# A recurrent scan on one core: one tanh per stream's step, 64-column state products, and a fixed order on PE

## The chip, the cores and the metric

The kernel runs on 1 core of a Trainium2 chip. The metric is device time in microseconds (us) of one execution. All arithmetic is fp32. In the trace every fp32 matrix product appears as two LDWEIGHTS and two MATMUL instructions, called its two passes here.

## The reference

The whole program is four layers of attention-like mixing and mixture-of-experts on 8 sequences of 256 tokens with 128 features. The change lies in the first layer's mixing alone, a nonlinear recurrence with 16 heads of 64 states and 8 features:

```
def _L0_attn_ref(tokens, norm_w, a, b, c, skip, w_out, b_out):
    ...
    x = tokens * jax.lax.rsqrt(ms + EPS) * norm_w
    x = x.reshape(B, T, H, D)            # 8, 256, 16, 8
    a_t = jnp.tanh(a)                    # 16 heads, 64 x 64
    state0 = jnp.zeros((B, H, S), dtype=tokens.dtype)

    def step(state, x_t):
        state = jnp.tanh(jnp.einsum('bhs,hst->bht', state, a_t) + jnp.einsum('bhd,hds->bhs', x_t, b))
        mixed = jnp.einsum('bhs,hsd->bhd', state, c) + skip[None] * x_t
        return (state, mixed)
    ...
    _, outs = jax.lax.scan(step, state0, xs)
    ...
    return tokens + outs @ w_out.T + b_out
```

The 256 steps are strictly one after another: each needs the tanh of the one before. The state of a step is 8 x 16 x 64 numbers. All later layers work on the normalised sum that this layer gives, so none of them can start before the scan's results are there.

## The kernel before, in words

The tokens are held in four groups of 512 (`g` of `NG`). `l0_attn` loads its weights, takes the tanh of `a`, clears the state tiles (L188), scales and transposes the tokens (L190 to L209) into `xd` (the input of the products, spread over head pairs) and `xnT` (for the skip term), and then runs the scan.

The 16 heads are arranged as 8 stacks of two heads. A stack's two heads share the 128 partitions: 64 states of one, 64 of the other. Stacks 0 to 3 are stream `h` = 0, stacks 4 to 7 stream `h` = 1; the two streams are independent, so that one can be on PE while the other is on ACT. Even and odd steps (`u`) pair the heads in two different ways, so that what leaves the products of one step has the arrangement that the next one needs.

A block is 16 steps (`TB`). For each block and stream a PSUM bank (`us`, pool `ps_s`, four banks) holds the sums of 16 steps.

- Input products (L224): for a block, 32 products with 32 output columns (a quarter of the array, `cols`) and 128 moving columns write b times x for all 16 steps at once.
- State products (L239): in each step and stream, eight products of 128 x 32 weights (half a head's features of one stack each) with 16 moving columns, added to the same bank. Four of them stand side by side on the four column quarters of PE's array.
- Tanh (L248): two ACTIVATEs of 64 partitions x 32 elements per step and stream. Each writes only the half of the partitions and the half of the state tile that its head owns; the other halves stay zero from the memset, which makes the state block-diagonal and keeps a stack's two heads apart in a 128-row product.
- Output products (L259): after a block, 16 products with 32 output columns and 128 moving columns give c times the state for the block, into `pm` in a bank of a lane's pool `ps`.
- DVE adds the skip term (L269, L270), and after the scan L280 multiplies `outsT` with the output weights.

What order the instructions take on an engine is decided by a scheduler, which works with its own estimate of each instruction's duration; the program's text only gives the dependencies. So before the change the input and output products stand between the state products wherever the scheduler saw room, often 20 and more in a row. `tc.add_manual_dep`, wrapped by `behind`, adds an order by hand; before the change it is used for some DMAs alone. Behind the scan come the router and the experts of the first layer (L301 and L306 are their products, L308 their gate), further attention layers, and the routed experts (L565 and L575 their products, L569 their gate).

Of the kernel before, what the change touches and what calls it, by code (L numbers as in the profile page):

```python
# [42 lines left out]
def tile_post_ln_blocks(ctx: ExitStack, tc: tile.TileContext, I, out: bass.AP):  # L43
# [10 lines left out]
    def bank(pool):  # L54
        return pool.tile([P, 512], F32, tag=pool.name, name=pool.name)
# [103 lines left out]
    def l0_attn(x):  # L159

        TB = 16
        cols = [slice(32 * c, 32 * c + 32) for c in range(4)]
        low, high = slice(0, 64), slice(64, 128)
        with ExitStack() as es:
            wp = es.enter_context(tc.tile_pool(name="l0w", bufs=1))
            wk = es.enter_context(tc.tile_pool(name="l0k", bufs=2))
            a_sb = load(wp, "L0_a")  # L170
            b_sb = load(wp, "L0_b")
            c_sb = load(wp, "L0_c")
            normw = load(wp, "L0_norm_w")
            normd = load(wp, "L0_norm_d")
            skip = load(wp, "L0_skip")
            woT = load(wp, "L0_w_outT")
            bout = load_row(wp, "L0_b_out")
            S.activation(a_sb, a_sb, AF.Tanh)

            xnT = wp.tile([P, T // 2, 2, B], F32, tag="xnT", name="xnT")  # L180
            xd = wp.tile([P, T // 2, 2, 2, B], F32, tag="xd", name="xd")
            outsT = wp.tile([P, B, T], F32, tag="outsT", name="outsT")
            states = []
            for h in range(2):
                states.append([])
# [24 lines left out]

            ps_m = es.enter_context(tc.tile_pool(name="ps_s", bufs=4, space=bass.MemoryType.PSUM))
            prev = [None, None]
            for blk in range(T // TB):
                ts = slice(blk * TB // 2, (blk + 1) * TB // 2)
                st = [states[h][blk % 2] for h in range(2)]
# [4 lines left out]
                for u in range(2):  # L220
                    for h in range(2):
                        for s in range(2):
                            for c in range(4):
                                PE.matmul(  # L224
                                    us[h][cols[c], s, u].rearrange("p t e b -> p t (e b)"),
                                    lhsT=b_sb[:, u, 4 * h + 2 * s + c // 2, 32 * (c % 2) : 32 * (c % 2) + 32],
                                    rhs=xd[:, ts, u, :, :].rearrange("p t e b -> p t (e b)"),
                                    start=(u == 0 and s == 0),
                                    stop=False,
                                    skip_group_check=True,  # L230
                                )
                for t in range(TB):
                    v, u = t // 2, t % 2
                    for h in range(2):
                        if prev[h] is not None:
                            for s in range(2):
                                for c in range(4):
                                    k = 2 * s + c // 2
                                    PE.matmul(  # L239
                                        us[h][cols[c], s, u, v].rearrange("p e b -> p (e b)"),  # L240
                                        lhsT=a_sb[:, u, 4 * h + k, 32 * (c % 2) : 32 * (c % 2) + 32],
                                        rhs=prev[h][:, k].rearrange("p e b -> p (e b)"),
                                        start=False,
                                        stop=(t == TB - 1),
                                        skip_group_check=True,
                                    )
                        for e, half in enumerate((low, high)):
                            S.activation(  # L248
                                st[h][half, v, u, :, e, :].rearrange("p (s k) b -> p s k b", s=2),
                                us[h][half, :, u, v, :, :],  # L250
                                AF.Tanh,
                            )
                        prev[h] = st[h][:, v, u]

                pm = bank(lanes[blk % 2].ps)[:, : TB * 2 * B].rearrange("p (u t e b) -> p u t e b", u=2, t=TB // 2, e=2)
                for u in range(2):
                    for k in range(2):
                        for q, c in enumerate(cols):
                            PE.matmul(  # L259
                                pm[c, u].rearrange("p t e b -> p t (e b)"),  # L260
                                lhsT=c_sb[:, u, 2 * q + k, :],
                                rhs=st[q // 2][:, :, u, 2 * (q % 2) + k].rearrange("p t e b -> p t (e b)"),
                                start=(u == 0 and k == 0),
                                stop=(u == 1 and k == 1),
                                skip_group_check=True,
                            )
                for u in range(2):
                    o = outsT[:, :, blk * TB : (blk + 1) * TB].rearrange("p b (t u) -> p t u b", u=2)[:, :, u]
                    V.scalar_tensor_tensor(o, xnT[:, ts, u], skip, pm[:, u, :, 0], ALU.mult, ALU.add)  # L269
                    V.tensor_tensor(o, pm[:, u, :, 1], o, ALU.add)  # L270

            for g in range(NG):
                xb = wk.tile([P, 4, D], F32, tag="sq", name="xb")
                V.scalar_tensor_tensor(
                    xb, x[g], 2.0, bout.unsqueeze(1).to_broadcast([P, 4, D]), ALU.mult, ALU.add
                )
                ps = quarters(bank(lanes[g % 2].ps))
                for j in range(4):
                    i = 4 * g + j
                    PE.matmul(  # L280
                        ps[:, j, :],
                        lhsT=outsT[:, i // 2, (i % 2) * P : (i % 2) * P + P],
                        rhs=woT,
                        start=True,
                        stop=True,
                    )
                V.tensor_tensor(xb, ps, xb, ALU.add)
                mixed(lanes[g % 2], g, xb)
# [1097 lines left out]
```

## Time and profile before

| what | us |
|---|---|
| median of 3 runs | 2330.99 |
| lowest and highest of them | 2328.26, 2331.98 |
| the profiled execution's own time | 2149.32 |
| its span, first to last instruction | 2147.6 |
| PE busy in the span | 1785.1 (83%) |
| ACT busy in the span | 950.8 (44%) |
| DVE busy in the span | 1267.9 (59%) |
| mean granted TensorE clock in the span | 0.872 |

The profile is one execution; its own time is some 182 us below the three runs. Busy shares are averages over stages with different limits. In a line for a group of instructions stand the source line, the engine, the operation, what it writes and reads with partitions x elements, the count, then busy us and mean ns of one, then the idle time of the engine just before them and what ended most of it. PEld is PE's weight load, listed by itself. The ends of matmuls are modelled, since they run in a pipeline.

### The profile page before, as it was taken

To read this page: it belongs to the slowest core of one execution; us is meant where nothing else is said; L and a number is where in the kernel's file an instruction comes from. 1 tells how busy PE (TensorE), PEld (TensorE's weight loads), DVE (VectorE), ACT (ScalarE), POOL (GpSimd) and SP (SyncE) were. 2 spreads that over 40 slices of the span, in tenths; PEclk is the share of its full clock that TensorE was granted. 3 is DMA by queue.
4 is the path that set the end of the run, shared out by engine and by line. 5 is a ranking of instruction groups with operands and counts; after the bars stand their busy time and mean duration, and the time that the engine had idled before them with its cause. 6 is when DMAs were issued, how large, how long until landed. Compare 5 with 4: busy or idle time off the path is not lost.

```text
span 2147.6 us, 46517 instructions
## 1 busy us (share of the span) xinstructions
PE 1785.1 (83%) x18200; PEld 1188.6 (55%) x18200; DVE 1267.9 (59%) x4476; ACT 950.8 (44%) x2385; POOL 290.4 (14%) x307
## 2 busy tenths in 40 slices
PE   5888878997899999999879762676975989998787
PEld 4666654455555544654458541554753766665564
DVE  3000016586786765689636851565667988477754
ACT  5666664372464435652333310243432554444424
POOL 1000000000000000003731067721047000000000
PEclk8666668997899999999879975798996999999958
DMA  3000006950233352235479795787731000000000
GB/s 94 5 5 5 5 4 192 270 165 0 62 96 81 87 149 75 63 82 160 119 248 315 232 274 180 237 283 226 209 91 51 1 1 1 1 6 6 1 1 11
DMA packets 186523, 219.66 MB, mean 102 GB/s; under 512 B 52896, under 2 KB 132256, under 8 KB 186304
## 3 DMA queue, kind: packets, MB, share of 16 engines
q1 hardware_dynamic: 163136, 164.24, 26.4%
q0 software_dynamic: 12800, 33.57, 5.1%
q10 hardware_dynamic: 10368, 18.88, 2.3%
q8 instruction: 143, 2.34, 0.5%
q14 instruction: 76, 0.62, 0.1%
HBM read 152.07 MB, written 64.55 MB: 101 GB/s over the span
## 4 chain that ended last, share of the span: by engine, by line
PE 60%; DVE 11%; ACT 9%; DMA 8%; POOL 6%; issue 5%; SPq 0%; ACTq 0%; POOLq 0%; DVEq 0%
PE ps_o L301 8%; PE ps_m L306 7%; PE ps_m L311 5%; ACT st L248 5%; PE ps_s L239 4%; PE ps L128 4%; PE ps L1002 3%; POOL got L586 3%; POOL placed L484 3%; PE ps L996 3%; PE ps_o L575 2%; DMA got<-in_F_w_dram,ei 2%; DMA got<-made,pl 2%; PE ps_s L224 2%; PE ps L1122 2%
## 5 line engine op out<-in xcount | busy, mean ns | idle before, releaser
L239 PE MATMUL ps_s<-st,L_a 128*32 128x16 f32 x8160 | 200.9, 206 | 45.1 <-ACT st L248 22.4
L248 ACT ACTIVATE st<-ps_s 64x32 f32<-64x32 f32 x1024 | 196.5, 192 | 92.8 <-PE ps_s L239 59.2
L308 ACT ACTIVATE h<-ps_m 128x512 f32<-128x512 f32 x196 | 116.1, 597 | 241.8 <-PE ps_m L306 222.3
L239 PEld LDWEIGHTS ps_s<-st,L_a 128*32 128x32 f32 x8160 | 159.2, 134 | 89.7 <-ACT st L248 72.3
L306 PE MATMUL ps_m<-xT,wg 128*128 128x512 f32 x384 | 197.8, 598 | 7.5 <-ACT h L308 7.5
L301 PE MATMUL ps_o<-h,wd 128*128 128x512 f32 x384 | 197.6, 599 | 7.0 <-DVE h L314 7.0
L455 POOL DMA_INDIRECT got<-in_F_w_dram,ei x32 | 30.7, 959 | 1121.4 <-DVE ei L442 971.4
L269 DVE SCALAR_TENSOR_TENSOR outsT<-xnT,L_skip,ps 128x64 f32<-128x64 f32 x32 | 10.3, 323 | 272.1 <-PE ps L259 255.5
L314 DVE TENSOR_TENSOR h<-h,bc 128x512 f32<-128x512 f32 x192 | 131.3, 686 | 45.9 <-ACT h L308 39.1
L484 POOL DMA_INDIRECT placed<-x,pl x128 | 126.3, 986 | 121.6 <-DVE pl L480 83.2
L586 POOL DMA_INDIRECT got<-made,pl x128 | 122.7, 959 | 126.3 <-DMA made<-ob 87.6
L311 PE MATMUL ps_m<-xT,wu 128*128 128x512 f32 x256 | 135.0, 609 | 4.1 <-ACT h L308 3.7
L575 PE MATMUL ps_o<-w,h 64*64 64x128 f32 x1152 | 94.0, 310 | 42.1 <-DVE h L570 29.2
L301 PEld LDWEIGHTS ps_o<-h,wd 128*128 128x128 f32 x384 | 72.1, 192 | 92.7 <-issue 62.5
L306 PEld LDWEIGHTS ps_m<-xT,wg 128*128 128x128 f32 x384 | 71.0, 191 | 91.7 <-issue 65.0
L312 DVE TENSOR_TENSOR h<-h,ps_m 128x512 f32<-128x512 f32 x132 | 90.0, 682 | 48.7 <-PE ps_m L311 43.7
L575 PEld LDWEIGHTS ps_o<-w,h 64*64 64x64 f32 x1152 | 73.7, 153 | 60.1 <-DVE h L570 41.6
L996 PE MATMUL ps<-nT,A_w 128*128 128x512 f32 x192 | 97.9, 623 | 10.1 <-DVE hT L998 7.3
L1002 PE MATMUL ps<-A_w,hT 128*128 128x128 f32 x768 | 101.1, 287 | 4.0 <-DVE hT L998 4.0
L1002 PEld LDWEIGHTS ps<-A_w,hT 128*128 128x128 f32 x768 | 95.2, 200 | 15.5 <-DVE hT L998 7.9
L565 PE MATMUL ps_m<-xg,w 128*64 128x64 f32 x1152 | 57.9, 252 | 50.2 <-DMA w<-further 22.7
L577 ACT COPY ob<-ps_o 128x512 f32<-128x512 f32 x72 | 42.2, 586 | 127.2 <-PE ps_o L575 124.9
(356 smaller groups left out, 3617.4 us busy)
## 6 DMA issues: line engine op xcount, KB each, us to landing
bc<-comb SPq DMA_DIRECT2D x128, 256.0 KB
placed<-zero SPq DMA_DIRECT2D x72, 256.0 KB
xb<-placed SPq DMA_DIRECT2D x72, 256.0 KB
made<-ob ACTq DMA_DIRECT2D x72, 256.0 KB
further<-got SPq DMA_DIRECT2D x32, 512.0 KB
w<-in_F_wg_dram SPq DMA_DIRECT2D x40, 256.0 KB
w<-in_F_wd_dram SPq DMA_DIRECT2D x40, 256.0 KB
bc<-comb SPq DMA_DIRECT2D x16, 512.0 KB
```

What stands on the lines that cost most here:

```text
L239: PE.matmul(us[h][cols[c], s, u, v].rearrange("p e b -> p (e b)"), lhsT=a_sb[:, u, 4 * h + k, 32 * (c % 2) : 32 * (c % 2) + 32], rhs=prev[ ...
L248: S.activation(st[h][half, v, u, :, e, :].rearrange("p (s k) b -> p s k b", s=2), us[h][half, :, u, v, :, :], AF.Tanh,)
L301: PE.matmul(acc[g], lhsT=w, rhs=h, start=begin, stop=end, skip_group_check=True)
L306: PE.matmul(pg, lhsT=wg, rhs=xT[g], start=True, stop=True)
L308: gate = S.activation(h, pg, func).ins
L311: PE.matmul(pu, lhsT=wu, rhs=xT[g], start=True, stop=True)
L314: V.tensor_tensor(h, h, bc[:, i * GT : (i + 1) * GT], ALU.mult)
L484: i = G.indirect_dma_start(placed[h][:, :], bass.IndirectOffsetOnAxis(rw[:, j, c : c + 1], 0), x[g][:, j, :], None).ins
L575: PE.matmul(po[k, i // 2, :], lhsT=h[k, i // 2, :], rhs=wd[k, i // 2, :], start=True, stop=True)
L586: G.indirect_dma_start(got[:, c, :], None, made[g // 2][:, :], bass.IndirectOffsetOnAxis(row[g][:, j, c : c + 1], 0))
L996: PE.matmul(ph, lhsT=w1[:, f * P : (f + 1) * P], rhs=nT, start=True, stop=True)
L1002: PE.matmul(po[:, j, :], lhsT=hT[:, f, j * P : (j + 1) * P], rhs=w2[:, f, :], start=(f == 0), stop=(f == 3),)
```

## The change

- The state tile of a stream and block has 2056 columns instead of 1024: each group of 8 columns that a head owns (`z` = 1) now has 8 columns of zeros ahead of it (`z` = 0), and 8 zeros close the tile.
- A stack's state product takes all 64 features of a head in one: 128 x 64 weights and 32 moving columns, on one of two halves of PE's array (`sides`). The moving columns are a window on the state tile that starts 8 columns later for one half than for the other, so that each half's own head meets numbers and the other meets zeros. There are four such products per step and stream.
- Since the sums of the foreign head are zero, one tanh of 128 partitions x 64 elements serves a stream's step.
- A bank now holds 8 steps (`HB`), and its 16 input products have 64 output columns and 64 moving columns.
- The first step too runs its state products, on a zero state.
- PE's order in the scan is written out: `in_turn` puts every state, input and output product behind the one before. In each step come stream 0's four products, two input products for the next half block, stream 1's four products, and after every fourth step four output products of the block before. The last block's outputs follow after the scan.

```diff
         TB = 16
         cols = [slice(32 * c, 32 * c + 32) for c in range(4)]
-        low, high = slice(0, 64), slice(64, 128)
+        sides = [slice(0, 64), slice(64, 128)]
...
-                    t = wp.tile([P, TB // 2, 2, 4, 2, B], F32, tag=f"st{h}{k}", name=f"st{h}{k}")
+                    t = wp.tile([P, TB * 4 * 32 + 8], F32, tag=f"st{h}{k}", name=f"st{h}{k}")
                     (V if h else G).memset(t, 0.0)
...
+            HB = TB // 2
+            def inputs(n):
                 us = [
-                    bank(ps_m).rearrange("p (s u t e b) -> p s u t e b", s=2, u=2, t=TB // 2, e=2)
+                    bank(ps_m).rearrange("p (t u s e f b) -> p t u s e f b", t=HB // 2, u=2, s=2, e=2, f=2)
                     for h in range(2)
                 ]
...
+                def product(u, h, s, c):
+                    return PE.matmul(
+                        us[h][sides[c], :, u, s, :, c, :],
+                        lhsT=b_sb[:, u, 4 * h + 2 * s + c, :],
+                        rhs=xd[:, n // 2 : (n + HB) // 2, u, :, :],
+                        start=(u == 0 and s == 0),
+                        stop=False,
+                        skip_group_check=True,
+                    )
...
+            def outputs(blk):
...
+                def product(u, k, q):
+                    return PE.matmul(
+                        pm[cols[q], u],
+                        lhsT=c_sb[:, u, 2 * q + k, :],
+                        rhs=st[q // 2][:, :, u, 2 * (q % 2) + k, :, 1, :],
...
+                def finish():
...
+            us, todo = inputs(0)
+            for f in todo:
+                f()
+            last = None
+            def in_turn(m):
+                nonlocal last
+                if last is not None:
+                    behind(m.ins, last, "steps in turn")
+                last = m.ins
+            outs, finish = [], None
+            prev = [states[h][1][:, (TB - 1) * 128 :] for h in range(2)]
+            for n in range(T):
+                t, blk = n % TB, n // TB
+                if t == 0 and blk:
+                    outs, finish = outputs(blk - 1)
+                if n % HB == 0:
+                    now, ins = us, []
+                    if n + HB < T:
+                        us, ins = inputs(n + HB)
+                for h in range(2):
+                    for s in range(2):
+                        for c in range(2):
+                            k = 2 * s + c
+                            in_turn(PE.matmul(
+                                now[h][sides[c], n % HB // 2, n % 2, s].rearrange("p e f b -> p (e f b)"),
+                                lhsT=a_sb[:, n % 2, 4 * h + k, :],
+                                rhs=prev[h][:, 32 * k + 8 * (1 - c) : 32 * k + 8 * (1 - c) + 32],
+                                start=False,
+                                stop=(n % HB == HB - 1),
+                                skip_group_check=True,
+                            ))
+                    st = states[h][blk % 2]
+                    S.activation(
+                        st[:, t * 128 : t * 128 + 128].rearrange("p (k e z b) -> p k e z b", k=4, e=2, z=2)[:, :, :, 1],
+                        now[h][:, n % HB // 2, n % 2].rearrange("p s e f b -> p (s e) f b"),
+                        AF.Tanh,
+                    )
+                    prev[h] = st[:, t * 128 : t * 128 + 136]
+                    if h == 0:
+                        more, ins = ins[:2], ins[2:]
+                    else:
+                        more, outs = (outs[:4], outs[4:]) if n % 4 == 3 else ([], outs)
+                    for f in more:
+                        in_turn(f())
+                    if finish and not outs:
+                        finish()
+                        finish = None
+            outs, finish = outputs(T // TB - 1)
+            for f in outs:
+                f()
+            finish()
...
```

In the changed file the state products are line 297, the tanh line 306, the input products line 224 still, the output products line 250, and DVE's two operations for them lines 262 and 263; everything behind the scan lies 54 lines further down.

More of the change, by code (lines that the diff above doesn't have):

```diff
@@ L211, in l0_attn @@
             ps_m = es.enter_context(tc.tile_pool(name="ps_s", bufs=4, space=bass.MemoryType.PSUM))
[L212 to L215, printed above, removed]
+            HB = TB // 2
+            def inputs(n):
                 us = [
-                    bank(ps_m).rearrange("p (s u t e b) -> p s u t e b", s=2, u=2, t=TB // 2, e=2)
+                    bank(ps_m).rearrange("p (t u s e f b) -> p t u s e f b", t=HB // 2, u=2, s=2, e=2, f=2)
@@ L218, in l0_attn @@
                     for h in range(2)
                 ]
[L220 to L264, printed above, removed]
-                                skip_group_check=True,
-                            )
@@ L267, in l0_attn @@
[L267 to L270, printed above, removed]
+                def product(u, h, s, c):
[7 more added lines that the diff above has]
+                    )
@@ new lines, in inputs @@
+                todo = [
+                    (lambda a=(u, h, s, c): product(*a))
+                    for u in range(2) for h in range(2) for s in range(2) for c in range(2)
+                ]
+                return us, todo
+            def outputs(blk):
+                st = [states[h][blk % 2][:, : TB * 4 * 32] for h in range(2)]
+                st = [t.rearrange("p (t u k e z b) -> p t u k e z b", t=TB // 2, u=2, k=4, e=2, z=2) for t in st]
+                pm = bank(lanes[blk % 2].ps)[:, : TB * 2 * B].rearrange(
+                    "p (u t e b) -> p u t e b", u=2, t=TB // 2, e=2
+                )
+                ts = slice(blk * TB // 2, (blk + 1) * TB // 2)
+                def product(u, k, q):
[3 more added lines that the diff above has]
+                        rhs=st[q // 2][:, :, u, 2 * (q % 2) + k, :, 1, :],
+                        start=(u == 0 and k == 0),
+                        stop=(u == 1 and k == 1),
+                        skip_group_check=True,
+                    )
+                def finish():
+                    for u in range(2):
+                        o = outsT[:, :, blk * TB : (blk + 1) * TB].rearrange("p b (t u) -> p t u b", u=2)[:, :, u]
+                        V.scalar_tensor_tensor(o, xnT[:, ts, u], skip, pm[:, u, :, 0], ALU.mult, ALU.add)
+                        V.tensor_tensor(o, pm[:, u, :, 1], o, ALU.add)
+                return [
+                    (lambda a=(u, k, q): product(*a)) for u in range(2) for k in range(2) for q in range(4)
+                ], finish
@@ new lines, in l0_attn @@
+            us, todo = inputs(0)
[27 more added lines that the diff above has]
+                                stop=(n % HB == HB - 1),
+                                skip_group_check=True,
+                            ))
[4 more added lines that the diff above has]
+                        AF.Tanh,
+                    )
+                    prev[h] = st[:, t * 128 : t * 128 + 136]
[8 more added lines that the diff above has]
+                        finish = None
```

## The prediction

> **What bounds the kernel now.** I read the page's table of slices first, then busy time by stretch, then the chain of waits inside the scan, last the groups of instructions that resemble the new ones.
>
> ```profile
> PE   5888878997899999999879762676975989998787
> PEclk8666668997899999999879975798996999999958
> ...
> L239 PE MATMUL ps_s<-st,L_a 128*32 128x16 f32 x8160 | 200.9, 206 | 45.1 <-ACT st L248 22.4
> L248 ACT ACTIVATE st<-ps_s 64x32 f32<-64x32 f32 x1024 | 196.5, 192 | 92.8 <-PE ps_s L239 59.2
> ```
>
> A slice is 53.7 us, so slices 2 to 6 are the scan: PE looks busy, but its rows count latency, ACT is busy for 0.6 of them by the same table, and the granted clock is 0.6. By the timeline its first tanh starts at 28.91 and its last ends at 315.38: 286.5 us, or 1.119 us for each of 256 steps. Nothing else of weight runs there, and every later stage needs its result, so a microsecond taken from the scan is one taken from the span. Two pieces of the chain show what a plain step is made of, at full and at half clock (start, length, what; us):
>
> ```profile
> 103.66 0.20 ACT st L248
> 103.86 0.02 issue
> 103.88 0.20 ACT st L248
> 104.08 0.02 issue
> ```
>
> ```profile
> 73.24 0.46 PE ps_s L239 x16
> 73.70 0.02 issue
> 73.72 0.02 ACTq L248
> 73.74 0.04 issue
> 73.79 0.20 ACT st L248
> 73.98 0.02 issue
> 74.00 0.20 ACT st L248
> 74.20 0.04 issue
> ```
>
> At full clock the tanh follow each other with no PE between (the next at 104.10 and 104.31, the next step's first at 104.57): ACT is the bound, 0.91 us a step. At half clock it is one stream's own loop: 0.46 (PE's 16 passes, two for each of 8 products) + 0.09 (issue, and a separate wait for ACT's own semaphore) + 0.42 (two tanh) + 0.04 = 1.01. The other 0.15 us of the mean step comes from the input and output products, which stand in clumps. So the clock matters. Each stretch below is about one step of the granted clock (stretch, length, PE busy (x), PEld busy (x), DVE, ACT, POOL, PEclk, DMA):
>
> ```profile
> 32.61:36.02 3.41, 2.54 (x128) 1.75 (x128) 0.00 (x0) 2.84 (x16) 0.00 (x0) 1.00 0.02 5
> 131.59:135.00 3.41, 3.08 (x118) 2.72 (x114) 0.00 (x0) 2.14 (x12) 0.00 (x0) 0.50 0.02 5
> 138.42:141.83 3.41, 2.66 (x133) 2.00 (x126) 0.00 (x0) 2.56 (x14) 0.00 (x0) 1.00 0.03 7
> 312.50:315.91 3.41, 3.28 (x78) 2.34 (x80) 0.00 (x0) 1.49 (x8) 0.00 (x0) 0.50 0.02 5
> ```
>
> The first was followed by half clock, the third by full; the second stayed at half, the fourth rose. Busy time doesn't sort them; the share in which moving columns stream does. A pass of 512 columns takes 0.43 us at full clock (L306: two passes in 0.86 in the chain), so 0.84 ns a column, 1.68 at half; four column tiles share the array. First: 128 x 16/4 x 0.84 = 0.43 of 3.41, 0.13. Third (100 passes of L239, 33 of L224 with 128 columns): 0.36. Second (92 of L239, 25 of L259): 0.57 at half. Fourth (48 of L239, 28 of L259, 2 of L280): 0.66. So the clock falls somewhere between shares 0.13 and 0.36 and rises between 0.57 and 0.66.
>
> **The change part by part.** Sums are against the profiled execution: 2149.32 us, span 2147.6. The median of the runs shown is 2330.99, 8.5% more; no view shows where those 182 us lie. The gain in them lies between the plain difference and one stretched by 1.085.
>
> *Tanh.* Two of 64x32 become one of 128x64. L248 takes 192 ns for 32 elements, and
>
> ```profile
> L569 ACT ACTIVATE h<-ps_m 128x256 f32<-128x256 f32 x72 | 27.7, 384 | 111.5 <-PE ps_m L565 91.0 <-DMA A_w<-in_A_w_dram 4.6 <-DMA made<-ob 4.1
> ```
>
> 384 for 256, so 64 take about 0.22 us: 0.20 less in each stream's loop, and ACT needs 0.5 us a step with its waits, no longer a bound. The separate wait stays (448 of 512 tanh wait on PE and on ACT; before, 450 of 1024).
>
> *State products.* Eight products of 32 columns with 16 moving become four of 64 with 32, so 8 passes in four pairs. The twin is L565, 128x64 weights with 64 moving, at full clock:
>
> ```profile
> 1107.59 0.68 PE L565 MATMUL ps_m<-xg,w 128*64 128x64 f32 x14
> ```
>
> ```profile
> 1107.16 0.25 PEld L575 LDWEIGHTS ps_o<-w,h 64*64 64x64 f32 x4
> 1107.59 0.54 PEld L565 LDWEIGHTS ps_m<-xg,w 128*64 128x64 f32 x14 [0.17 <-issue]
> ```
>
> 0.68 less the last pass's 0.22 is 0.46 for eight pairs: 0.058 a pair, set by the weights. Four pairs with the first load put the last start near 0.20; with a pass's 0.20 and the 0.04 that PE's piece in the chain ends after it, 0.44 against 0.46 before at half clock. The loop becomes 0.44 + 0.09 + 0.22 + 0.04 = 0.79 us. Bounds for the burst, 0.37 (no pacing) and 0.50 (every pair at twice): 18 us of scan down, 15 up.
>
> *Fixed order.* Each step now issues: stream 0's burst, two input products, stream 1's burst, and after every fourth step four output products. Bursts hold PE 0.20 each, the inputs 0.12 (two pairs at 0.058): 0.52 of 0.79, which fits. Each burst's first load waits for its own tanh; behind a waiting stream 1 stands stream 0's next burst, which isn't due before 0.79, so that costs nothing. Outputs do: they use 32-column tiles between bursts of 64. The weight loader idles 0.17 with no releaser as L575 (64x64) gives way to L565 (128x64) above; some 0.09 of it is after L575's columns have streamed. [...] From stream 1's last start (0.33 + 0.20): 0.03 streaming + 0.09 + 0.25 (a load, two passes of 128 columns) + 0.09 puts the next burst at 0.99 instead of 0.79: 0.05 us a step. [...] In the scan's tail a switch to 128x128 at half clock idles the loader 0.38, which would give 0.10. I take 0.05: 0.84 us a step, 215 us for 256.
>
> *Start and end.* The four memsets double (DVE 0.91 to 1.8 each, POOL 0.94 to 1.9), and DVE takes two xb operations (1.3 for both) earlier. Most hides behind the load of norm_d, which ends at 16.28, and the scaled copies of ACT; the last copies wait 0.97 for DVE already, so I add 1.5 (0 to 3). Of the input products only 16 stand ahead of the first burst, 32 passes or 1.7 us at half clock from 25.57: the first burst is at 28.8. Until the clock rises, 1.5 more. The end is 28.8 + 1.5 + 215 = 245 against 315.4: 70 us saved. The last block's outputs and DVE's four operations follow as before; the other blocks' DVE work hides in the scan, and if it didn't, a block's 1.2 us would show. No DMA, SP or POOL queue of the scan is moved.
>
> *Behind the scan.* The scheduler issues the same work; PE's order is unchanged up to about half of its later instructions (routed experts of the second half), then some shift by up to 61 places; SP swaps a few loads for later layers with the zeroing of placed. I count 0, with 15 us either way.
>
> Profiled execution: 2149 - 70 = 2079. Median: 2331 - 70 to 2331 - 76; I say 2258.
>
> **The rivals.**
>
> *The clock stays at half (slower).* Then pairs are 0.116 apart: burst 0.69 to its end, loop 1.04, but PE itself needs 0.42 + 0.23 + 0.42 = 1.07 a step, and outputs with two drains 0.86 in four: 1.29 a step, 330 us, so 44 more than now: about 2376. Streaming per step is 8 x 32 state + 128 input + 64 output columns = 448, 0.75 us at half clock: a share of 0.58, just where the trace shows neither sure rise nor stay. At full clock it is 0.377/0.84 = 0.45, above the 0.36 that stayed. So it is bistable, and the first burst decides: with 1.7 us of inputs in a 3.41 us window the share is about 0.75 if all lie in one, below 0.6 if split. The decisive point is a step of 1.12, some 60% of the scan at half. For a rise: any window that catches more inputs and outputs than average passes 0.62, and one rise is enough. [...]
>
> *Half in part.* Falls in some blocks, as now: a mean step near 1.0, 256 us, 30 saved less the start: 2303.
>
> *PE's order saves nothing, later stages lose.* If the new loop were 0.79 but every burst waited for the inputs ahead of it (0.12 twice) and the reordered tail lost 15: 1.08 a step, 10 saved, 15 lost, 2336. The 0.52 of 0.79 speaks against it.
>
> **How the numbers follow.** Full clock 0.75: 2258, own range 2220 to 2300 (18 burst, 13 drains, 15 tail, partly added). Half in part 0.12: 2303. Half throughout 0.09: 2376. Nothing gained 0.04: 2336. Range 2215 to 2325: it leaves out the half-clock case, the last one and the ends of the first. Faster by over 0.2%, about what a measurement of this kernel can tell from no change, 0.86; within 0.02; slower 0.12.
>
> **What would show it.** Right: PEclk near 1.0 through the scan, the last tanh near 245, tanh about 220 ns x512, a plain loop of 0.79 in the chain with every fourth step near 1.0, loader idle before L250 and the next L297 with no releaser. Wrong: PEclk 0.5 with PE as releaser throughout, a loop without the 0.2 at outputs, or stages behind the scan that differ by over 15 us.

## The result, and the profile after

The changed kernel takes 2294.87 us (median of 4 runs) where the kernel before takes 2329.62 on the same chip: a ratio of 0.9847, interval 0.9823 to 0.9871, or 35 us less. Of its four runs three lie between 2291.58 and 2297.73; the fourth, 2388.87, is left out of the ratio, and its cause is a finding below.

The page of the changed kernel, PE's busy tenths and granted clock by slice, then the two groups that replace L239 and L248:

```profile
PE   6999799779999999738993044577945899997798
...
PEclk9999899889999999958996555688976998998857
...
L297 PE MATMUL ps_s<-st,L_a 128*64 128x32 f32 x4096 | 197.7, 223 | 6.3 <-ACT st L306 0.3
...
L306 ACT ACTIVATE st<-ps_s 128x64 f32<-128x64 f32 x512 | 114.3, 223 | 109.4 <-PE ps_s L297 78.2
```

The scan is slices 1 to 4 now and its clock is full. ACT's tanh are half as many at 223 ns, and ACT's idle time ends on PE. By the timeline the first tanh starts at 29.76 and the last ends at 251.49: 221.7 us against 286.5, and what follows starts 64 us earlier. A piece of the chain of waits with one step that carries output products (start, length, what):

```profile
120.28 0.03 issue
120.31 0.42 PE ps_s L297 x8
120.73 0.14 PE ps_s L224 x4
120.88 0.21 PE ps_s L297 x8
121.08 0.36 PE ps L250 x8
121.44 0.35 PE ps_s L297 x8
```

By the starts of the tanh a plain step takes 0.808 us and the one after output products 1.061. The page that was shown of before came from an execution of 2149.32 us, this one from 2291.58; so behind the scan these two pages must not be subtracted from each other. That needs both kernels on one chip.

### The profile page after: what moved, and what is told of

It reads as the page before. It is cut to its first block, busy times and chain, and to the rows that moved or that the text cites. A ratio compares the mean times of both kernels' runs of the same rounds, so it can differ in the third digit from the quotient of the medians.

```text
span 2289.8 us, 37891 instructions
## 1 busy us (share of the span) xinstructions
PE 1815.9 (79%) x14136; PEld 1198.2 (52%) x14136; DVE 1268.2 (55%) x4476; ACT 865.8 (38%) x1873; POOL 290.0 (13%) x307
## 4 chain that ended last, share of the span: by engine, by line
PE 62%; DVE 12%; DMA 9%; another core or an unknown queue 8%; ACT 4%; issue 4%; SPq 1%; POOL 0%; ACTq 0%; DVEq 0%; POOLq 0%
PE ps_s L297 7%; PE ps_o L355 7%; PE ps_m L360 6%; PE ps_m L365 4%; PE ps L128 4%; PE ps L1056 3%; PE ps L1050 3%; PE ps_o L629 2%; DMA w<-further 2%; PE ps L1176 2%; PE ps L1160 2%; PE ps L991 2%; PE ps_s L224 2%; DMA further<-got 2%
## 5 line engine op out<-in xcount | busy, mean ns | idle before, releaser
L355 PE MATMUL ps_o<-h,wd 128*128 128x512 f32 x384 | 202.4, 612 | 18.1 <-DVE junk L556 7.5
L360 PE MATMUL ps_m<-xT,wg 128*128 128x512 f32 x384 | 203.3, 613 | 8.8 <-ACT h L362 7.5
L297 PE MATMUL ps_s<-st,L_a 128*64 128x32 f32 x4096 | 197.7, 223 | 6.3 <-ACT st L306 0.3
L297 PEld LDWEIGHTS ps_s<-st,L_a 128*64 128x64 f32 x4096 | 161.4, 137 | 39.0 <-issue 10.5
L365 PE MATMUL ps_m<-xT,wu 128*128 128x512 f32 x256 | 140.9, 633 | 41.3 <-DVE junk L556 32.2
L306 ACT ACTIVATE st<-ps_s 128x64 f32<-128x64 f32 x512 | 114.3, 223 | 109.4 <-PE ps_s L297 78.2
L538 POOL DMA_INDIRECT placed<-x,pl x128 | 125.2, 978 | 118.3 <-DVE pl L534 79.9
L1050 PE MATMUL ps<-nT,A_w 128*128 128x512 f32 x192 | 104.5, 663 | 17.4 <-DVE hT L1052 9.7
L624 DVE SCALAR_TENSOR_TENSOR h<-h,ps_m 128x256 f32<-128x256 f32 x72 | 29.9, 415 | 151.4 <-ACT h L623 120.3
```

The costliest lines, as they stand in the source:

```text
L297: in_turn(PE.matmul(now[h][sides[c], n % HB // 2, n % 2, s].rearrange("p e f b -> p (e f b)"), lhsT=a_sb[:, n % 2, 4 * h + k, :], rhs=prev ...
L306: S.activation(st[:, t * 128 : t * 128 + 128].rearrange("p (k e z b) -> p k e z b", k=4, e=2, z=2)[:, :, :, 1], now[h][:, n % HB // 2, n % ...
L355: PE.matmul(acc[g], lhsT=w, rhs=h, start=begin, stop=end, skip_group_check=True)
L360: PE.matmul(pg, lhsT=wg, rhs=xT[g], start=True, stop=True)
L365: PE.matmul(pu, lhsT=wu, rhs=xT[g], start=True, stop=True)
L538: i = G.indirect_dma_start(placed[h][:, :], bass.IndirectOffsetOnAxis(rw[:, j, c : c + 1], 0), x[g][:, j, :], None).ins
```

## The experiments

### Both kernels again, on one chip

> The kernel before, profiled again. Theory A (the first profile of before, 2149 us in its own execution, showed an execution without the stalls that the timed ones have behind the scan): the scan takes 286 us as then, but the own time of this execution is near 2330 us, and the 180 us between lie behind the scan, in waits of DVE and ACT near POOL's indirect transfers, as in the profile after (its jumps at 1013-1030 and 1245-1255 us of before's time). Rival R1 (executions under the profiler are simply shorter for this kernel): own time near 2150 us again, no such stalls, and then the change itself brings the stalls that the profile after shows.

> The changed kernel, profiled again. Theory A: own time 2285 to 2300 us; scan 221 us (first tanh near 30, last near 251 us); laid beside e0_before step for step, the first instruction behind the scan is 63 us earlier, and about 29 of these 63 us are given back further on. Where they are given back tells the cause: at POOL's indirect bursts (a stall that meets other work), or in the last third, where the scheduler's order of the tail differs (L3 stages). Rival R1: 2150 to 2300 us, with the stalls absent in e0_before only.

On this chip the kernel before took 2155 us (median of 23 runs), and e0_before 2161.67. In all later runs, on three chips, it took 2155 to 2162, and in the first measurement, on a chip that the record does not number, 2330. The profiler does not make an execution shorter: e0_before, profiled, took as long as the timed ones, and the first profile of the changed kernel (2291.58) is one of the timed executions of the first measurement. So A was wrong about e0_before, and R1 had the number right and the reason wrong. Where the 175 us lie is seen by laying one changed kernel beside itself on two chips (the first profile, and e11_after_again below, 2120.51 us): equal within 2 us up to 950 us, then 63 us later by 975 (46 by 1100), 124 by 1200, 145 by 1400 and 171 from 1700 on. The waits of the first profile, in 950 to 1030 and in 1227 to 1311 us (us in total, times, longest):

```profile
DVE junk L556 <- remote: 26.7, 11, 3.9
ACT h L362 <- remote: 24.9, 2, 15.6
...
ACT ob L631 <- remote: 63.2, 2, 54.2
```

DVE and ACT wait for something that the profile can't name, beside POOL's indirect transfers (L538). e0_before, e1_after and e11_after_again have no such wait at all. Both kernels are slower by as much on that chip (2330 and 2295, on the others 2155 and 2120), so it is no part of the change; that the kernel before loses it in the same place is inferred, since no profile of it comes from that measurement. What it is was not tried.

e1_after was the surprise: 2217.7 us. Its scan took 317.6 us, 1.067 us for a plain step and 1.80 after output products, at a PEclk row that shows nothing:

```profile
PEclk9999998999899999999889965888978899988857
```

The trace's record of the clock has its first entry at 353.8 us in this execution (at 31.6 us in the first profile of the changed kernel), and the page takes what lies before a first entry as full speed. The products tell more. The groups of the first profile in 29.6 to 31.4 us, then in 60 to 100, and of e1_after in 60 to 100 (the second number after the bar is the mean ns):

```profile
L297 PE MATMUL ps_s<-st,L_a 128*64 128x32 f32 x32 | 2.2, 290 | 0.0
```

```profile
L297 PE MATMUL ps_s<-st,L_a 128*64 128x32 f32 x744 | 36.0, 222 | 1.2
```

```profile
L297 PE MATMUL ps_s<-st,L_a 128*64 128x32 f32 x518 | 34.7, 291 | 0.0
```

Until its clock rose the first profile ran at 290 ns a pass too. e1_after never left that pace: pairs of passes start 107 ns apart there, 58 to 59 in the other at full clock. The whole scan ran at half clock.

### What decides the clock

In 3.41 us stretches laid back from the first entry of each record I counted the share in which columns stream, as the prediction does. The stretch ahead of the rise had 0.69 in the first profile and in e11_after_again and 0.75 in e4_clumps. In e1_after no stretch of the scan had more than 0.66 (most 0.58 to 0.61), and none rose. That points to the burst ahead of the scan as what raises the clock, if enough of it falls into one stretch. e7_warm puts more of it there:

```diff
+            warm, last = bank(ps_m), None
+            for i in range(2):
+                m = PE.matmul(warm, lhsT=ident, rhs=b_sb[:, 0, :, :]..., start=True, stop=True)
+                behind(m.ins, shuffled, "after the last transposes")
             us, todo = inputs(0)
             for f in todo:
-                f()
+                behind(f().ins, m.ins, "after the warming products")
```

> The changed kernel with two 128x512 products of the identity with L0_b (results unused) on PE between the last transposes and the first input products, where PE is idle from 23.4 to 27.3 us. Theory D (whether the scan runs at the full or at half the clock is decided by how much of one 3.41 us window the burst ahead of the scan fills: .69 raised it, .63 did not, and the steady scan at half clock fills only .58 to .63): every execution rises before the scan, none is 80 to 95 us longer than the others, total within 3 us of the changed kernel's short executions. Rival R4 (it is a property of the execution, not of the burst): of some 4 executions one or two are 80 to 95 us longer again.

2121.16, 2121.42, 2121.44 and 2123.98 us, ratio 0.9841 (0.9795 to 0.9887): D held. The clock's record starts at 24.9 us and the scan at 28.2.

> The changed kernel itself once more, for how often its scan stays at half the clock where nothing warms PE ahead of it. Theory D: two kinds of executions, near 2120 and near 2215 us on a chip where before takes 2155, with nothing between. Rival R4': one kind only, near 2120.

2117.11, 2120.51, 2123.77 and 2210.72: two kinds, nothing between. Over the unwarmed kernels of this study (the changed one, e4_clumps, e5_tail_of_before) 6 of 20 executions were of the long kind; with the two products ahead (e7, e8, e12 and e13 below) 0 of 20. If the two products did nothing, so uneven a split would come about once in a hundred. Two of the six have a profile, and both show the whole scan at the slow pace; the other four are told by their length. The share is a rough measure, though: in e5_tail_of_before's profiled execution a stretch ahead of the scan had 0.72 and the clock did not rise, and in e10_order_alone below it rose at 0.52 and 0.54.

The clock's record moves in steps: the first profiles of the two kernels have 106 and 92 entries, each at 0.50 or 1.00, and each but the last of a profile lasts 3.413 us or a whole multiple of it. Whether the place of the burst against these steps lets one program fall to either side is not shown: no run here moves that place alone, and e5_tail_of_before's 0.72 speaks against its being the whole cause.

### Where the rest of the gain went

The scheduler gives both kernels the same work behind the scan in two orders. e5 and e6 exchange them: each engine's instructions behind the scan are chained in the other kernel's order (one memset of DVE apart).

```diff
+def chain(nc, tc):
+    ...
+    for name, packed in TAIL.items():
+        ...
+        for a, b in zip(order, order[1:]):
+            tc.add_manual_dep(own[b], own[a].name, behind, reason="as in the other kernel")
```

> The changed kernel's scan, with everything behind the scan in the order in which each engine has it in the kernel before (the scheduler is held to it by order-only dependencies). Theory C (the scheduler's other order of the last third, the L3 stages, costs 25 us of the scan's 62): an execution whose scan runs at the full clock keeps the whole gain, 60 to 70 us, ratio .968 to .974 to before on a chip where before takes 2155 us (.970 to .975 where it takes 2330). Rival R3 (the gain is given back because later stages start earlier and meet other transfers or another clock phase, whatever the order): ratio .982 to .987 as for the changed kernel. An execution whose scan stays at half the clock is 95 us longer than either.

> The kernel before, its scan untouched, with everything behind the scan in the order of the changed kernel. Theory C: 20 to 30 us slower than before, ratio 1.009 to 1.014, all of it in the last third (from about 1400 us on). Rival R3: within 5 us of before, ratio .998 to 1.002.

e5: 0.972 (0.9676 to 0.9764), 60 us under before. e6: 1.0101 (1.0052 to 1.015), 22 us over it. C held from both sides, and R3 fell. Laid beside e0_before, e6 is 3 to 13 us early up to 1800 us and 20 late at the end. The last stretch of e0_before, then of e6 (stretch, length, PE busy, PEld, DVE, ACT, POOL, PEclk, DMA share, GB/s):

```profile
1775.00:2160.00 385.00, 341.31 (x1976) 224.89 (x1974) 240.50 (x953) 154.57 (x316) 0.00 (x0) 0.88 0.01 4
```

```profile
1775.00:2180.00 405.00, 360.60 (x1930) 236.27 (x1928) 229.96 (x906) 146.93 (x301) 0.00 (x0) 0.82 0.01 3
```

About as many PE instructions take 20 us longer, at a lower clock. By the timeline, in the order of before the last two token groups go through the last layers side by side: the 64 passes on hT of both stand at 2044 to 2058, and the score products of both follow from 2080 to 2144. In the order of after one group has its 32 passes at 2041 to 2045, the other at 2066 to 2070; the score products run from 2073 to 2162. That the stagger lowers the clock, and the clock makes the loss, is what these rows suggest; it was not tried by itself.

e8_warm_tail takes both, the two products ahead and the tail's order of before:

> Both: the two products ahead of the scan, and the order of the kernel before behind it. Theories C and D together: every execution 60 to 70 us under before (ratio .968 to .974), the first version to beat both kernels in all executions. By R3: .982 to .987. By R4: a spread of 80 to 95 us between its executions.

2082.46 to 2092.19 us in six runs, ratio 0.9677 (0.9641 to 0.9713), 70 us under before: faster than both kernels in every run. e7 and e8 differ in the order behind the scan alone, ran on one chip, and had no long execution; so the order costs 34 us there (2121.43 against 2087.15), where e7 against e5 gives 26 and e6 against before 22. The last stretch of e8, then of e7:

```profile
1710.00:2085.00 375.00, 334.34 (x1943) 220.80 (x1941) 233.57 (x910) 150.20 (x305) 0.00 (x0) 0.88 0.01 4
```

```profile
1710.00:2119.00 409.00, 362.18 (x1963) 239.12 (x1961) 234.79 (x944) 149.69 (x308) 0.00 (x0) 0.83 0.01 3
```

Again the order of after brings no more PE work and a lower clock.

### What inside the scan carries the gain

The fixed order taken out of the changed kernel (the scheduler places all products):

```diff
-                if last is not None:
+                if False:
                     behind(m.ins, last, "steps in turn")
```

> The changed kernel without its fixed order: in_turn holds nothing, so the scheduler places input and output products. Theory B (the merged tanh and 64-column products alone carry the gain, and the fixed order only removes a tenth): scan 225 to 240 us, total 2295 to 2315 us, ratio to before .985 to .995. Rival R2 (the fixed order carries the gain): input products of a half block stand in one lump ahead of the stream's step, 16 x 0.1 us or so each 8 steps, and the tilings alternate more often: scan 250 to 285 us, total 2320 to 2360 us. A tail placed in another order can move either by 30 us.

Ratio 1.0006 (0.9981 to 1.0032): B fell. The scan is 283.1 us. Plain steps take 0.81 as with the order, but clumps of products make others 1.9 to 2.8, and the clock is at half for 94 us of it; how the loss divides between the two was not tried. The waits in 29 to 315 us, of e2_free and of the changed kernel (its first profile):

```profile
ACT st L306 <- PE ps_s L297: 164.4, 355, 2.8
```

```profile
ACT st L306 <- PE ps_s L297: 78.2, 259, 2.0
```

The tanh split in two again, in e8_warm_tail:

```diff
-                    S.activation(st[:, ...], now[h][:, ...], AF.Tanh)
+                    for side in sides:
+                        S.activation(st[side, ...], now[h][side, ...], AF.Tanh)
```

> e8_warm_tail with the one tangent of a stream's step cut into two again, of 64 partitions each (products of 64 columns and the fixed order kept). Two of about 0.2 us in a row lengthen a stream's own chain (0.81 us in the changed kernel) by 0.2 us, and ACT carries four of them a step. Theory E (the single tangent is a necessary part of the gain): step 1.00 to 1.05 us, scan 255 to 275 us, 35 to 50 us slower than e8_warm_tail, ratio to before .985 to .992. Rival R5 (PE's fixed order is the whole gain, ACT has room): step within 0.05 us of 0.86, ratio .967 to .973.

1.0297 (1.0217 to 1.0376): slower than before, scan 342.6 us. E's direction held, its size did not, because the clock fell. e14 adds four products behind the second stream in each step without outputs, which write to an unused bank:

> e9_two_tanh with four more products of 64 columns in each step behind the second stream (results unused), for PE's share. In e9_two_tanh PE filled .29 to .39 of its 3.41 us windows at the full clock, and the clock fell to half after 44 us and stayed there for 294 us. Theory G (the second tangent's own price is 0.2 us a step, and the rest of e9's 122 us came from the clock): clock full throughout, step 1.03 to 1.10, scan 265 to 285 us. Rival R7 (the clock is not what made e9 slow): half a microsecond more PE work a step only adds, scan 340 us or more.

Scan 277.0 us, plain step 1.045: more work on PE, 66 us less. The stretches of e9_two_tanh, then of e14:

```profile
29.00:70.00 41.00, 37.13 (x851) 30.11 (x850) 1.09 (x4) 34.71 (x160) 0.00 (x0) 1.00 0.01 3
...
110.00:240.00 130.00, 129.93 (x2046) 111.16 (x2044) 6.52 (x24) 80.73 (x372) 0.00 (x0) 0.50 0.01 2
```

```profile
110.00:200.00 90.00, 89.42 (x2318) 77.55 (x2314) 5.49 (x20) 72.16 (x332) 0.00 (x0) 1.00 0.02 4
```

G held (in one execution): the second tanh's own price is about 277 - 221 = 56 us, and e9's other 66 are the clock. e9 itself says nearly the same: until its clock fell, 49 us after its first tanh (not the 44 of the expectation), its plain steps took 0.985 to 1.045. With this longer loop PE streams in 0.29 to 0.39 of a stretch, and the clock fell; the changed kernel at 0.41 to 0.46 (0.30 to 0.37 from 240 us on, where its input products are at an end) kept it. The share alone does not decide it, as the next run shows too.

The fixed order alone, on the kernel before (32-column products and two tanh stay; the two warming products, and the tail's order of before):

```diff
-            for blk in range(T // TB):
-                ...
+            for n in range(T):
+                ...  # stream 0, two input products, stream 1, four output products every 4th step
+                in_turn(PE.matmul(now[h][cols[c], s, u, v]..., lhsT=a_sb[:, u, 4 * h + k, 32 * (c % 2) : ...], ...))
```

> The kernel before with the fixed order alone: its products of 32 columns and its two tangents stay, but PE takes stream, two input products, stream, and four output products every 4th step in a fixed order; with the two products ahead of the scan and the tail's order of before as in e8_warm_tail. Theory E: the two tangents bound it, .91 us a step at the full clock or 1.01 at half: scan 235 to 262 us against 286 before, ratio .977 to .989. Rival R5: step near 0.86, scan 220 us, ratio .967 to .973. If the order gains nothing here, ratio .998 to 1.002.

0.9991 (0.9951 to 1.0031), scan 280.6 us. Its median step is 0.909, the two-tanh bound that E counted on, but every few steps one takes 1.4 to 2.1. The chain at such a step:

```profile
41.73 0.04 issue
41.77 0.31 PE ps_s L302 x14
42.09 0.78 issue
42.87 0.18 PE ps_s L302
```

In the middle of a burst, with no wait for any semaphore, PE stands still for 0.78 us. The waits in 29 to 309 us put 60 of these to PE's weight loader:

```profile
PEld ps_s L302 <- issue: 32.5, 60, 1.1
```

In the kernel before, in 29 to 315 us, there are few:

```profile
PEld ps_s L239 <- issue: 4.2, 10, 1.0
```

The standstills, more than the clock, make the 48 us that e10's scan takes over 256 x 0.909: its clock was full for all but 22 us of the scan. It stayed full although columns stream in only 0.16 to 0.29 of a stretch, where e9 lost it at 0.29 to 0.39. The stretch from 31 to 122 us:

```profile
31.00:122.00 91.00, 68.23 (x3131) 45.22 (x3119) 4.37 (x16) 63.64 (x333) 0.00 (x0) 1.00 0.02 5
```

A step of this kernel issues 76 PE instructions (64 for states, 8 for inputs, 4 for outputs on average); 256 x 76 in 280.6 us are 69 a us. The kernel before has as many in 286.5: 68. e15_narrow makes it plain, by cutting the 64-column products of e8_warm_tail in two (those for the states are shown; the input products are cut alike):

```diff
-                            in_turn(PE.matmul(now[h][sides[c], ...], lhsT=a_sb[:, n % 2, 4 * h + k, :], ...))
+                            for i in range(2):
+                                in_turn(PE.matmul(
+                                    now[h][cols[2 * c + i], ...], lhsT=a_sb[:, n % 2, 4 * h + k, 32 * i : 32 * i + 32], ...))
```

> e8_warm_tail with its single tangent and its fixed order, but with each product of 64 columns cut into two of 32: the same streaming time on PE's array side by side, twice the instructions. Theory H (PE gets no more than 67 to 69 instructions a us over a longer stretch, as in the kernel before and in e10_order_alone, which stood still 60 times for 0.5 to 1 us with nothing to wait for): 256 x 84 / 68 = 316 us, scan 300 to 320 us, with such standstills. Rival R8 (the width of a product costs nothing): steps of .81 to .90, scan 221 to 235 us.

Scan 309.6 us in its one execution, 256 x 84 instructions: 69 a us again. H held. Its waits in 29 to 338 us, and the line of the queue that brings instructions (packets, MB, share):

```profile
PEld ps_s L312 <- issue: 69.5, 62, 1.7
...
PEld ps_s L234 <- issue: 19.6, 17, 1.8
```

```profile
q8 instruction: 152, 2.49, 0.5%
```

There are 80 standstills over 0.5 us, 1.2 us each on average; 76 of the 79 distances between them are exactly 256 PE instructions. The trace's records of that queue point to what PE stood waiting for. In the scan the queue brings 84 packets of 16,384 bytes, one for each 256 of its 256 x 84 PE instructions, and each of the 80 standstills ends 1.1 to 1.6 us after such a packet has landed. e15's clock is at half for 138 us of its scan, but that is not the limit: at full clock (52.96 to 56.37 us) as at half (49.55 to 52.96) 128 products start in 3.41 us. The two lines above sum to 89 us, and the scan is 88 us longer than e8's. In the scans of the first profiles the queue brings 76 such packets (the kernel before) and 44 (the changed one): again one for each 256 of 256 x 76 and 256 x 44 PE instructions. e10 and e15 stand still at 69 instructions a us; the changed kernel issues 50 and has no standstill over 0.5 us in its scan. The kernel before, at 68, has 19 of them, 13 us together, so most of its scan's time has other causes.

### The output products

Eight behind every 8th step instead of four behind every 4th:

```diff
-                        more, outs = (outs[:4], outs[4:]) if n % 4 == 3 else ([], outs)
+                        more, outs = (outs[:8], outs[8:]) if n % 8 == 7 else ([], outs)
```

> The changed kernel with its output products in lumps of 8 every 8th step instead of 4 every 4th: half as many changes between the 64- and the 32-column tilings. If the +0.25 us of each 4th step is mostly the two changes of tiling (0.15 to 0.20 us), the scan is 32 x 0.15 to 32 x 0.20, 5 to 6 us, shorter (221 to 215 us). If it is the four products themselves, or their wait for the bank, the lump costs twice as much and the scan stays within 1 us of 221. Total: before's ratio .982 to .987 by the first, .985 by the second.

Ratio 0.9838 (0.9782 to 0.9894), scan 221.7 us: nothing saved. Eight cost 0.47 us in one step, four 0.25. Halving the changes of tiling makes no difference.

e12_inputs_aside and e13_outputs_between move products inside e8_warm_tail:

```diff
-                        more, ins = ins[:2], ins[2:]
+                        take = (3, 3, 2, 0)[n % 4]
+                        more, ins = ins[:take], ins[take:]
```

> e8_warm_tail with the input products kept off the steps that carry output products (3, 3, 2, 0 in place of 2, 2, 2, 2 of each four steps). If PE's own time is what a 4th step's extra 0.25 us is, taking two input products (0.117 us) off it saves up to 0.1 x 64 = 6 us: ratio to before .964 to .967, step of the 4th 0.95. If it is the output products' place between one stream's burst and the next one's start, nothing: the same scan within 2 us of e8_warm_tail.

The 4th step is 1.178 instead of 1.061 and the scan 227.9 us: longer by 6.8, which neither case had. A likely reason is that three products between the streams start the second stream later, and that the output products behind it lie deeper in the way of the first one's next burst; it was not tried by itself. e13 keeps the 3, 3, 2, 0 and puts the outputs between the streams, in the step without inputs (`if n % 4 == 3` under `h == 0`):

> e8_warm_tail with the four output products put between the two streams' bursts, in the steps that carry no input products (3, 3, 2, 0). Where they stand now, behind the second stream, they lie in front of the first stream's next burst, and that step takes 1.06 us instead of .81. Theory F (it is the place: PE is busy only .58 of the .81 us; between the streams they push the second stream back once, by some .25 us, and then lie in that gap in each later step): steps .81 to .83 throughout, scan 208 to 214 us against 221, total 8 to 13 us under e8_warm_tail, ratio to before .960 to .965. Rival R6 (four output products cost .25 us wherever they stand, by the two changes of tiling): scan 219 to 223 us, ratio .967 to .972.

Scan 215.5 us, 4th step 0.944: better by 5.6, a half of what F counted, and R6 fell. The total, 2087.66 us with runs from 2073.14 to 2103.77 (0.9698, 0.9656 to 0.9741), can't be told from e8_warm_tail's; where the rest of the runs' spread comes from stays open.

## Why the prediction was right or wrong, point by point

- *Tanh*: right. 0.22 was 0.223, and its separate wait for ACT's own semaphore stayed (450 of 512).
- *State products and the loop*: 0.79 was 0.808, 5 us over 256 steps. The burst's pieces, 0.44, are 0.42 and 0.03 in the chain.
- *Fixed order, outputs*: +0.20 in each fourth step was +0.25, 3 us in all. The size was near, its terms are not borne out: no run shows the drains of the array that the two 0.09, the rival's 0.86 and the range's 13 us stand for. In the first profile of the changed kernel PE's loader idles 0.20 us ahead of the burst behind the outputs (10.5 us in 53 waits with no releaser), and ahead of the outputs no wait is listed; e4 halved the changes of tiling for nothing (0.47 us for eight products, 0.25 for four), and e13 changed the price by place (a 4th step of 0.944 instead of 1.061).
- *Start and end*: the last tanh was to end near 245 and ended at 251.5. Together the scan saved 64 us where 70 were forecast.
- *Behind the scan* is the step that failed: "I count 0, with 15 us either way". It is 34 (e7 against e8), 26 (e7 against e5, 0.9841 and 0.972) or 22 (e6 against before). 64 less 22 to 34 leaves 30 to 42 us, and 35 were measured. The prediction saw PE's order shift by up to 61 places and took it for nothing because the work was the same. Its own sign of being wrong, stages behind the scan that differ by over 15 us, is what came. The measured 2294.87 lies near the 2303 of *half in part* by chance: the scan's clock was full.
- *Median less 70 to 76*: the 182 us between the profiled execution and the runs are one chip's waits behind the scan (171 us found there in the changed kernel). They do not stretch the changed scan: 221.7 us there and 222.4 in e11_after_again.
- *The rival at half clock* came as described (the whole scan of e1_after), was near in its price, and too small in its chance: 0.09 forecast, 6 of 20 executions. A step was 1.29 in the forecast and 1.237 in the run, the scan 330 and 317.6. That the total was 56 us slower (2217.7 against 2161.67) where 44 were forecast is in part luck: the scan alone lost 33, and the rest was lost behind it, where 0 was counted. The prediction's "any window that catches more inputs and outputs than average passes 0.62, and one rise is enough" failed: stretches of 0.62 to 0.66 went by all through the scan without a rise.
- *The share* fails as a measure of its own. e10_order_alone kept full clock at shares of 0.16 to 0.29, below the 0.36 that the prediction counted as safe and below the 0.29 to 0.39 that e9_two_tanh lost it at, so at best the share compares kernels with products of one width. Pauses of PE don't sort the two either: in e9's scan no two PE instructions start over 0.5 us apart, and its clock fell, while e10, with standstills of up to 1.1 us, kept it. What does decide it stays open.
- *Half in part* did not occur in any profile of the changed kernel, nor did the case that the order saves nothing. The order is needed (e2), but so are the single tanh (e9) and the wide products (e15): each of the three left out alone gives all of the scan's gain back (in e9 the second tanh itself takes 56 of the 64 us, the clock the rest and more).

## What to carry to other kernels

A change that shortens one stage lets the scheduler order the later ones anew, and that order can be worth a third to a half of the gain (22 to 34 of 64 us here); hold it still (chain each engine as it was) before a stage's change is judged, and after. Where PE runs small products in a dependent loop, count its instructions a microsecond, for they met a ceiling here (69 in the two kernels that reached it), and look at the pace of its products, for such a loop can run at half clock without a gap. Two useless products just ahead of the loop settled the clock for all of it where the loop then held it (0 of 20 executions of the long kind, 6 of 20 without them), and did not in e9.

## What the runs showed of the hardware that was not expected

- PE's instructions came at 69 a us at most over a whole scan, in two kernels of different form (e10, e15); in e15 a packet of 16,384 bytes comes for each 256 of them, and PE goes on 1.1 to 1.6 us after one has landed, 80 times.
- A scan of 221 us can stay at half clock from end to end, at 318 us, with no two PE instructions starting over 0.5 us apart; and the page then shows full clock, because the record has no entry before 353.8 us (e1_after).
- More PE work shortened a loop: 342.6 us without, 277.0 with four extra products a step (e9, e14).
- A loop that streams in 0.16 to 0.29 of each 3.41 us kept full clock for over 90 us (e10), and one at 0.29 to 0.39 lost it after 49 us (e9).
- One chip added some 175 us to either kernel; in the changed one they lie in waits near POOL's indirect transfers that the profile gives to another core or an unknown queue.
